# A graph layer bound by its gathers: first loads in one queue by need, two blocks' messages ahead of the weights, x + b_e copied one chunk in each block

## The chip, the cores and the metric

The kernel runs on one core of a Trainium2 chip. The metric is the device time of one execution in microseconds (us), of which a median over several runs is given. The profile is of one further execution. Engines are named as in the profile: PE is TensorE (PEld its weight loads), DVE is VectorE, ACT is ScalarE, POOL is GpSimd, SP is SyncE; SPq and ACTq stand for the DMA issues of SP and ACT.

## The reference

There are N = 8192 nodes of C = 256 channels and E = 131072 edges, sorted by destination. All data is fp32.

```python
ea = edge_attr @ w_e + b_e                       # 64 -> 256 per edge
msg = relu(x[src] + ea)
agg = segment_sum(msg, dst, num_segments=N)
t = x + agg
h_local = relu(t @ w1 + b1) @ w2 + b2
h_local = bn(h_local + x, bn1_g, bn1_b)
# attention inside groups of 32 nodes, 4 heads of 64
q, k, v = split((x.reshape(256, 32, 256) @ in_w.T + in_b), 3)
o = softmax(q k^T / 8) v
h_attn = bn(o @ out_w.T + out_b + x, bn2_g, bn2_b)
out = h_local + h_attn
out = out + (relu(out @ m_w1 + m_b1) @ m_w2 + m_b2)
result = layernorm(x + bn(out, bn3_g, bn3_b))
```

## The kernel before

**Edges.** The edges are worked in 128 blocks of 1024 (`NB`, `BE`). For a block, `gather` (L133) issues eight indirect DMAs from GpSimd (L138), each of 128 rows of 1 KB, into the buffer `xs`, of which there are four; `load_edges` (L148) issues four loads of 128 KB from SyncE into `ea` (two buffers). VectorE transposes `ea` into `eaT` (L169), TensorE multiplies by `w_e` into two two-bank PSUM tiles `pe` (L459), VectorE adds the gathered rows to make `msg` (L487, two instructions a block), and ScalarE applies the relu in place (L491). A gather of block b + 4 reuses the buffer of block b and so waits for the message of block b. `edge_hot` (L496) makes one-hot matrices, `edge_sums` (L510) and `edge_place` (L528, L538) sum two blocks' messages by destination and add them to the transposed nodes `xT`.

**x + b_e.** The bias `b_e` is added to all edges. For the first 20 blocks (`NX`) TensorE adds it with further matmuls into `pe` (L467), and the gathers read x itself. Meanwhile the kernel writes a copy xb = x + b_e to DRAM: load (L553), add on VectorE (L558), store (L559). From block 20 on gathers read xb and the matmuls at L467 fall away. The copies are cut by `steps` (L543): a step per two blocks, of one to three chunks of 512 nodes, in buffers shared with the dense layers. A step is loaded in one pair of blocks and added and stored in the next.

**Nodes.** The nodes are worked in 16 chunks of 512: `attention_front` (load xn at L276, transposes L283, q and k at L294), `attention_back` (v at L308, scores L325, softmax, output L360 and L372), and `dense` (all dense layers at L391, layernorm, store at L444). These generators are mixed into the blocks by `Work.run`, which spends a budget of estimated us per pair of blocks. Dense work begins only when all chunks are copied (`not xp_of`). The last 24 blocks are placed one by one with a list of expected gather times (`came`).

**Setup.** The source indices of the first two blocks come in by eight tiny loads (`srcd`, L64), so that GpSimd can start. Then the gathers and edge loads of blocks 0 and 1 are issued. All source indices are loaded as `srci_r` (L176), turned into fp32 (L193), transposed on TensorE (L197) and written to `srci` (L198), which gathers from block 2 on read. The destinations (`dsti_r`, L177) become `rel` and `wrow` (L232 to L267). Weights are transposed (L207).

**Order.** SyncE and ScalarE issue plain loads and stores; each of the two is one in-order queue, and across both eight completion semaphores are used in turn, so that a load waits for the one eight places before it to land. In the setup, a scheduler orders each engine's instructions. From the main loop on TensorE's order is as written (`manual_schedule`), and for the first 26 blocks (`NV`) VectorE's and ScalarE's as well (L661 to L667); after that the scheduler orders these two.

Of the kernel before, what the change touches and what calls it, by code (L numbers as in the profile page):

```python
# [18 lines left out]
P = 128  # L19
# [5 lines left out]
NH = 4  # L25
# [15 lines left out]
NV = 26  # L41
# [12 lines left out]
def gnn_kernel(ctx: ExitStack, tc: tile.TileContext, x, src, dst, edge_attr, w, out):  # L54
# [105 lines left out]
    load_edges(0)  # L160
    gather(1)
    load_edges(1)
# [7 lines left out]

    with tc.tile_pool(name="setup", bufs=1) as sp:


        srci_r = npool.tile([P, BE], I32, name="srci_r", tag="y")
        dsti_r = npool.tile([P, BE], I32, name="dsti_r", tag="h1")
        nc.sync.dma_start(srci_r, src.rearrange("(s e) -> s e", s=NB))  # L176
        nc.sync.dma_start(dsti_r, dst.rearrange("(s e) -> s e", s=NB))  # L177
        for h in range(2):
            nc.scalar.dma_start(we[h * ED : (h + 1) * ED, :], w["w_e"])
        nc.scalar.dma_start(be, w["b_e"][None, :].to_broadcast([P, C]))  # L180
        in_r = npool.tile([P, 3 * KC, C], FP, name="in_r", tag="m1")
        out_r = npool.tile([P, KC, C], FP, name="out_r", tag="vn")
        nc.scalar.dma_start(in_r, w["in_w"].rearrange("(o p) c -> p o c", p=P))
# [4 lines left out]
        nc.scalar.dma_start(out_r, w["out_w"].rearrange("(o p) c -> p o c", p=P))  # L188
        for b in range(2):
            edge_transpose(b)  # L190
            load_edges(b + 2)
        srcf = npool.tile([P, NH * TJ, EQ, QR], FP, name="srcf", tag="zT")
        nc.vector.tensor_copy(srcf, srci_r.rearrange("s (t r m) -> s t m r", r=QR, m=EQ))  # L193
        for h in range(NH):
            ps = bank()[:, : TJ * NB].rearrange("p (j s) -> p j s", j=TJ)
            for j in range(TJ):
                nc.tensor.transpose(ps[:, j, :], srcf[:, h * TJ + j].rearrange("s m r -> s (m r)"), ident)  # L197
            nc.vector.tensor_copy(srci[:, :, h * TJ : (h + 1) * TJ].rearrange("p s j -> p j s"), ps)  # L198

# [74 lines left out]
    def attention_front(n0, st, pool, bank):  # L274
        xn = st["xn"] = pool.tile([P, TN, C], FP, name="xn", tag="xn", bufs=4)
        nc.sync.dma_start(xn, x[ds(n0, CH), :].rearrange("(t p) c -> p t c", p=P))  # L276
        yield REST
# [170 lines left out]
    chunk = [{} for _ in range(NCH)]  # L448
    pe_of, msg_of, oh_of, newest = {}, {}, {}, {}

    def edge_products(b):

        eaT = eaT_of.pop(b).rearrange("p (h m) r -> p h (m r)", h=NH)
        for h in range(0, NH, 2):
            pe = bank2().rearrange("p i (u c) -> p i u c", u=2)
            for u in range(2):
                for i in range(2):
                    rows = slice(i * ED, (i + 1) * ED)
                    nc.tensor.matmul(  # L459
                        pe[:, i, u, :], eaT[rows, h + u], we[rows, :],  # L460
                        start=(b >= NX or u == 0), stop=(b >= NX), skip_group_check=True,
                    )
            if b < NX:
                for u in range(2):
                    for i in range(2):
                        rows = slice(i * ED, (i + 1) * ED)
                        nc.tensor.matmul(  # L467
                            pe[:, i, u, :], sel[rows, :], be[rows, :], start=False, stop=True, skip_group_check=True
                        )
            pe_of[b, h] = pe  # L470

    def next_edges(b):
        if b < NB:
            edge_transpose(b)
        if b + 2 < NB:
            load_edges(b + 2)

    def edge_messages(b):

        xs = xs_of.pop(b)  # L480
        msg = msg_of[b] = epool.tile([P, NH, TJ, C], FP, name="msg", tag="msg", bufs=3)
        n = 2 if b < NB - 1 else 1
        for h in range(0, NH, 2):
            pe = pe_of.pop((b, h))
            for u in range(0, 2, n):
                hs = slice(h + u, h + u + n)
                nc.vector.tensor_add(  # L487
                    msg[:, hs].rearrange("p u i c -> p i u c"), pe[:, :, u : u + n, :],
                    xs[:, hs].rearrange("p u i c -> p i u c"),
                )  # L490
                nc.scalar.activation(msg[:, hs], msg[:, hs], AF.Relu)  # L491

    def edge_hot(b):

        oh = oh_of[b] = epool.tile([P, TB, WN], FP, name="oh", tag="oh", bufs=2)
        nc.vector.tensor_tensor(  # L496
            oh,
            iota_n[:, None, :WN].to_broadcast([P, TB, WN]),
            rel[:, b, :, None].to_broadcast([P, TB, WN]),
            ALU.is_equal,  # L500
        )

    def edge_sums(blocks):

        pw = pps.tile([P, 2, C], FP, name="pw", tag="pw", bufs=1)
        for i, b in enumerate(blocks):
            msg, oh = msg_of.pop(b), oh_of.pop(b)
            for j in range(TJ):
                for h in range(NH):
                    nc.tensor.matmul(  # L510
                        pw[h * WN : (h + 1) * WN, i, :], oh[:, h * TJ + j, :], msg[:, h, j, :],
                        start=(j == 0), stop=(j == TJ - 1), skip_group_check=True,
                    )
        n = len(blocks)
# [3 lines left out]
        for i, b in enumerate(blocks):  # L518
            nc.vector.tensor_scalar(oh2[:, i, :], iota_n, wrow[:, b : b + 1], None, ALU.is_equal)
# [106 lines left out]
    with tc.manual_schedule(engines={PE}):  # L626
# [38 lines left out]
        while b < TAIL:  # L665
            if b == NV:
                early.close()  # L667
# [199 lines left out]
```

## Time and profile before

| what | value |
|---|---|
| median of 3 runs | 1328.58 us (1327.78 to 1329.9) |
| the profiled execution | 1331.09 us |
| its span | 1329.3 us |
| PE busy | 1195.2 us, 90% |
| POOL busy | 983.9 us, 74% |
| DVE busy | 784.9 us, 59% |
| ACT busy | 587.7 us, 44% |
| mean granted TensorE clock | 0.967 |
| DMA moved | 240.34 MB, mean 181 GB/s |

The span lies inside the profiled execution's own time. A row of a group reads: line, engine, operation, output and inputs, count, then total busy us and mean ns of one, then the engine's idle time just before these instructions and what ended most of it. A row of the order of time reads: start, duration, engine, line, operation, names, count, and in brackets the idle time just before and its releaser. Releasers are inferred; "issue" means that nothing which the profile shows was waited for. Successive instructions of one group are merged into one row.

### The profile page before, as it was taken

To read this page: it belongs to the slowest core of one execution; us is meant where nothing else is said; L and a number is where in the kernel's file an instruction comes from. 1 tells how busy PE (TensorE), PEld (TensorE's weight loads), DVE (VectorE), ACT (ScalarE), POOL (GpSimd) and SP (SyncE) were. 2 spreads that over 40 slices of the span, in tenths; PEclk is the share of its full clock that TensorE was granted. 3 is DMA by queue.
4 is the path that set the end of the run, shared out by engine and by line. 5 is a ranking of instruction groups with operands and counts; after the bars stand their busy time and mean duration, and the time that the engine had idled before them with its cause. 6 is when DMAs were issued, how large, how long until landed. Compare 5 with 4: busy or idle time off the path is not lost.

```text
span 1329.3 us, 21099 instructions
## 1 busy us (share of the span) xinstructions
PE 1195.2 (90%) x7795; PEld 741.0 (56%) x7795; DVE 784.9 (59%) x1339; ACT 587.7 (44%) x840; POOL 983.9 (74%) x1032
## 2 busy tenths in 40 slices
PE   2898989999998989899898988989898999999987
PEld 1566656556555556555555555545555555545655
DVE  4377555765756565755647465465646557575654
ACT  1343433454536454443435444354454444443433
POOL 6677777777777777777777777777777777777771
PEclk9899999999999989999999999989899999999998
DMA  7999966676667666666756666566566466656741
GB/s 204 320 267 299 260 199 169 169 199 167 181 160 196 157 181 167 171 177 165 190 150 185 160 176 171 157 181 167 170 169 199 138 169 186 166 163 159 192 129 47
DMA packets 148904, 240.34 MB, mean 181 GB/s; under 512 B 27934, under 2 KB 112188, under 8 KB 148028
## 3 DMA queue, kind: packets, MB, share of 16 engines
q0 software_dynamic: 49152, 134.28, 37.6%
q1 hardware_dynamic: 97196, 103.34, 28.9%
q10 hardware_dynamic: 2448, 1.32, 0.4%
q8 instruction: 63, 1.03, 0.3%
q14 instruction: 45, 0.37, 0.1%
HBM read 222.06 MB, written 16.78 MB: 180 GB/s over the span
## 4 chain that ended last, share of the span: by engine, by line
PE 38%; POOL 28%; issue 14%; DVE 9%; DMA 8%; ACT 2%; DVEq 0%; ACTq 0%; SPq 0%; POOLq 0%
POOL xs L138 28%; PE at L391 11%; PE pe L459 8%; DMA xs<-xb,srci 5%; PE at L294 5%; PE pw L510 4%; DVE msg L487 3%; PE l L528 3%; PE at L372 2%; PE pe L467 2%; PE at L308 1%; DMA xp<-in_x_dram 1%; PE at L360 1%; PE pe L325 1%; DMA in_r<-in_L_gnn_in_w_dram 1%
## 5 line engine op out<-in xcount | busy, mean ns | idle before, releaser
L138 POOL DMA_INDIRECT xs<-xb,srci x864 | 823.7, 953 | 263.2 <-issue 250.1
L491 ACT ACTIVATE msg<-msg 128x1024 f32<-128x1024 f32 (+1 forms) x258 | 270.0, 1049 | 435.5 <-DVE msg L487 432.6
L487 DVE TENSOR_TENSOR msg<-pe,xs 128x1024 f32<-128x1024 f32 (+1 forms) x258 | 305.7, 1199 | 155.4 <-DMA xs<-xb,srci 88.6
L459 PE MATMUL pe<-we,eaT 64*128 64x256 f32 x2048 | 271.0, 398 | 29.8 <-DVE msg L487 26.4
L459 PEld LDWEIGHTS pe<-we,eaT 64*128 64x128 f32 x2048 | 192.1, 191 | 118.5 <-issue 74.6
L138 POOL DMA_INDIRECT xs<-in_x_dram,srci x144 | 143.0, 993 | 48.8 <-issue 39.6
L169 DVE STREAM_TRANSPOSE eaT<-ea 128x512 f32<-128x512 f32 x128 | 90.1, 704 | 99.6 <-PE pe L459 70.9
L510 PE MATMUL pw<-msg,oh 128*32 128x256 f32 x2048 | 130.4, 389 | 6.6 <-DVE oh L496 5.0
L391 PE MATMUL at<-hA,mw 128*128 128x512 f32 (+2 forms) x304 | 123.9, 538 | 2.9 <-DVE hA L401 2.2
L294 PE MATMUL at<-xT,inT 128*128 128x512 f32 x256 | 120.9, 598 | 0.4 <-ACT xT L284 0.4
L391 PE MATMUL at<-m,mw 128*128 128x512 f32 (+2 forms) x304 | 117.5, 529 | 2.5 <-ACT qk L297 2.2
L510 PEld LDWEIGHTS pw<-msg,oh 128*32 128x32 f32 x2048 | 60.4, 111 | 69.1 <-issue 30.7
L528 PEld LDWEIGHTS l<-oh,ws 128*128 128x128 f32 x512 | 78.0, 196 | 28.4 <-issue 21.9
L528 PE MATMUL l<-oh,ws 128*128 128x160 f32 x512 | 87.9, 312 | 2.0 <-ACT ws L516 2.0
L391 PEld LDWEIGHTS at<-hA,mw 128*128 128x128 f32 x304 | 54.7, 196 | 50.5 <-issue 42.6
L391 PEld LDWEIGHTS at<-m,mw 128*128 128x128 f32 x304 | 54.2, 190 | 49.9 <-issue 44.5
L538 DVE TENSOR_TENSOR xT<-l,xT 128x96 f32<-128x96 f32 (+4 forms) x107 | 46.1, 452 | 54.2 <-PE l L528 53.9
L294 PEld LDWEIGHTS at<-xT,inT 128*128 128x128 f32 x256 | 47.0, 190 | 55.3 <-issue 51.0
L391 PE MATMUL at<-xT,w 128*128 128x512 f32 (+2 forms) x152 | 70.9, 606 | 6.9 <-DVE xT L538 6.9
L407 ACT ACTIVATE m<-at,vec 128x512 f32<-128x512 f32 (+2 forms) x76 | 46.8, 616 | 57.2 <-PE at L391 56.7
L297 ACT ACTIVATE qk<-at,vec 128x512 f32<-128x512 f32 x64 | 43.6, 684 | 62.6 <-PE at L294 62.4
L391 PE MATMUL at<-h,w 128*128 128x512 f32 (+2 forms) x152 | 64.2, 544 | 6.1 <-ACT h L398 6.1
(107 smaller groups left out, 1199.9 us busy)
## 6 DMA issues: line engine op xcount, KB each, us to landing
ea<-in_edge_attr_dram SPq DMA_DIRECT2D x512, 128.0 KB
xs<-xb,srci POOLq DMA_INDIRECT x864
xn<-in_x_dram SPq DMA_DIRECT2D x16, 512.0 KB
out_dram<-y SPq DMA_DIRECT2D x14, 512.0 KB
xp<-in_x_dram SPq DMA_DIRECT2D x10, 512.0 KB
xb<-xp SPq DMA_DIRECT2D x10, 512.0 KB
xp<-in_x_dram SPq DMA_DIRECT2D x3, 1024.0 KB
xb<-xp SPq DMA_DIRECT2D x3, 1024.0 KB
```

The lines of the kernel that those rows point to most:

```text
L138: nc.gpsimd.indirect_dma_start(out=xs[:, h, j, :], out_offset=None, in_=x if b < NX else xb[:, :], in_offset=bass.IndirectOffsetOnAxis(ap= ...
L169: nc.vector.transpose(eaT, ea[:, QR:].rearrange("p (g d) -> p g d", d=ED)[:, :, :QR])
L294: nc.tensor.matmul(ps, inT[:, k, o * P : (o + 1) * P], xT[:, k, :], start=(k == 0), stop=(k == KC - 1))
L297: nc.scalar.activation(qk[:, o, :], ps, AF.Identity, bias=v_("in_b", o))
L391: nc.tensor.matmul(ps, wt[:, k, o * P : (o + 1) * P], act[:, k, :], start=(k == 0), stop=(k == nk - 1))
L407: nc.scalar.activation(m1[:, o, :], layer(mw1, KC, o, hA), AF.Relu, bias=v_("m_b1", o))
L459: nc.tensor.matmul(pe[:, i, u, :], eaT[rows, h + u], we[rows, :], start=(b >= NX or u == 0), stop=(b >= NX), skip_group_check=True,)
L487: nc.vector.tensor_add(msg[:, hs].rearrange("p u i c -> p i u c"), pe[:, :, u : u + n, :], xs[:, hs].rearrange("p u i c -> p i u c"),)
L491: nc.scalar.activation(msg[:, hs], msg[:, hs], AF.Relu)
L510: nc.tensor.matmul(pw[h * WN : (h + 1) * WN, i, :], oh[:, h * TJ + j, :], msg[:, h, j, :], start=(j == 0), stop=(j == TJ - 1), skip_group_ ...
L528: nc.tensor.matmul(l2[:, k, i * NPB : i * NPB + WB], ws[:, i, k * P : (k + 1) * P], oh2[:, i, :], start=(i == 0 and k == 0), stop=(i == la ...
L538: newest["xT"] = nc.vector.tensor_add(xT, l2[:, :, a - n : z - n], xT).ins
```

## The change

Three things change in the order of the work; what is computed stays the same.

1. The first loads all go through SyncE, in this order: `srcd` (ScalarE still issues half of these), `srci_r`, edge loads of block 0, `w_e`, edge loads of block 1, `b_e`, `dsti_r`, the twelve vectors, `in_w`, nodes of chunk 0, `out_w`, nodes of chunk 1. Before, `srci_r` and `dsti_r` stood behind both blocks' edge loads, and ScalarE issued the weights.
2. The products and messages of blocks 0 and 1 are written in the setup, behind the index transposes and ahead of the weight transposes, where the scheduler orders the engines. The main loop leaves them out for these two blocks.
3. The copy of x + b_e goes by one chunk of 512 nodes in each block (`copy_step`), in four buffers in turn: load chunk i, add and store chunk i - 2. There are sixteen adds of 128x1024 where there were ten of that size and three of 128x2048.

Beside this the written order of VectorE and ScalarE in the first 26 blocks is taken out: the scheduler orders both throughout. TensorE's order stays written. The functions of the edge blocks move up in the file unchanged.

```diff
-NV = 26
...
     gather(0)
-    load_edges(0)
     gather(1)
-    load_edges(1)
...
+    def load_nodes(n0, st, pool):
+        xn = st["xn"] = pool.tile([P, TN, C], FP, name="xn", tag="xn", bufs=4)
+        nc.sync.dma_start(xn, x[ds(n0, CH), :].rearrange("(t p) c -> p t c", p=P))
...
         srci_r = npool.tile([P, BE], I32, name="srci_r", tag="y")
+        nc.sync.dma_start(srci_r, src.rearrange("(s e) -> s e", s=NB))
+        load_edges(0)
         dsti_r = npool.tile([P, BE], I32, name="dsti_r", tag="h1")
-        nc.sync.dma_start(srci_r, src.rearrange("(s e) -> s e", s=NB))
+        for h in range(2):
+            nc.sync.dma_start(we[h * ED : (h + 1) * ED, :], w["w_e"])
+        load_edges(1)
+        nc.sync.dma_start(be, w["b_e"][None, :].to_broadcast([P, C]))
         nc.sync.dma_start(dsti_r, dst.rearrange("(s e) -> s e", s=NB))
-        for h in range(2):
-            nc.scalar.dma_start(we[h * ED : (h + 1) * ED, :], w["w_e"])
-        nc.scalar.dma_start(be, w["b_e"][None, :].to_broadcast([P, C]))
...
-        nc.scalar.dma_start(in_r, w["in_w"].rearrange("(o p) c -> p o c", p=P))
         vec_r = npool.tile([nrows, P], FP, name="vec_r", tag="pr")
...
-        nc.scalar.dma_start(out_r, w["out_w"].rearrange("(o p) c -> p o c", p=P))
-        for b in range(2):
-            edge_transpose(b)
-            load_edges(b + 2)
+        nc.sync.dma_start(in_r, w["in_w"].rearrange("(o p) c -> p o c", p=P))
+        load_nodes(0, chunk[0], npool)
+        nc.sync.dma_start(out_r, w["out_w"].rearrange("(o p) c -> p o c", p=P))
+        load_nodes(CH, chunk[1], npool)
...
+        for b in range(2):
+            edge_transpose(b)
+            load_edges(b + 2)
+        edge_products(0)
+        next_edges(2)
+        edge_messages(0)
+        edge_products(1)
+        next_edges(3)
+        edge_messages(1)
...
-    steps = [[("m1", 0, 2), ("y", 2, 1)], [("h1", 3, 1), ("zT", 4, 1)], [("m1", 5, 2), ("y", 7, 1)],
-             [("h1", 8, 1), ("zT", 9, 1)], [("m1", 10, 2), ("y", 12, 1)], [("h1", 13, 1), ("zT", 14, 1)],
-             [("y", 15, 1)]]
...
+    XP = ("y", "h1", "zT", "m1")
...
+    def copy_step(i):
+
+        if i - 2 in xp_of:
+            xp = xp_of.pop(i - 2)
+            nc.vector.tensor_add(xp, xp, be[:, None, :].to_broadcast([P, TN, C]))
+            nc.sync.dma_start(rows(xb, i - 2), xp)
+        if i < NCH:
+            xp = xp_of[i] = npool.tile([P, TN, C], FP, name="xp", tag=XP[i % len(XP)])
+            nc.sync.dma_start(xp, rows(x, i))
...
-        early = ExitStack()
-        early.enter_context(tc.manual_schedule(engines={mybir.EngineType.DVE, mybir.EngineType.Activation}))
...
-            if b == NV:
-                early.close()
...
-            edge_products(b)
-            next_edges(b + 2)
-            edge_messages(b)
+            if b:
+                edge_products(b)
+                next_edges(b + 2)
+                edge_messages(b)
...
             work.run(0.3 * per)
-            copy_store(b // 2 - 1)
-            copy_load(b // 2)
+            copy_step(b)
             if sums:
                 edge_place(*sums)
                 placed, sums = sums[0][-1], None
             work.run(0.2 * per)
+            copy_step(b + 1)
```

## The prediction

> **What bounds the kernel now.** I first looked at engine totals, then at the costliest group, then at the waits of its engine and at single instructions in order of time.
>
> ```profile
> span 1329.3 us, 21099 instructions
> PE 1195.2 (90%) x7795; PEld 741.0 (56%) x7795; DVE 784.9 (59%) x1339; ACT 587.7 (44%) x840; POOL 983.9 (74%) x1032
> L138 POOL DMA_INDIRECT xs<-xb,srci x864 | 823.7, 953 | 263.2 <-issue 250.1
> ```
>
> TensorE looks like the bound at 90%, but it is not what sets the end. The gathers at L138 (GpSimd, "POOL") are 1024: 128 blocks of eight. Each takes 0.95 us, and 0.30 us of "issue" (waiting for nothing) lies before it. In order of time:
>
> ```profile
> 4.25 1.10 POOL L138 DMA_INDIRECT xs<-in_x_dram,srcd  x1 [2.65 <-issue]
> ...
> 1302.79 0.95 POOL L138 DMA_INDIRECT xs<-xb,srci  x1 [0.30 <-issue]
> ```
>
> From first to last gather are 1298.5 us. 1023 steps of 1.25 us are 1278.8 us, so only 19.8 us of this stretch is anything else. After it come 26.5 us of tail (1329.3 - 1302.8): the last landing, its message, sums and dense layers. A change of first loads and copies can win from the 19.8 us, not from TensorE's load. GpSimd's own waits name the large pieces:
>
> ```profile
> POOL xs L138 <- issue: 297.0, 967, 2.6
> POOL xs L138 <- DVE msg L487: 6.9, 13, 3.2
> ...
> POOL xs L138 <- DVE oh L519: 2.6, 4, 1.7
> ...
> POOL xs L138 <- DVE srci L198: 0.9, 1, 0.9
> ```
>
> (columns: total, times, longest). Nearly every other entry is the usual 0.30 us with a chance neighbour as releaser; I take the chain's long TensorE stretch before 880 us for the same, since no gather there starts late. The gathers that do:
>
> ```profile
> 23.16 1.80 POOL L138 DMA_INDIRECT xs<-in_x_dram,srcd  x1 [0.30 <-issue]
> 25.87 1.47 POOL L138 DMA_INDIRECT xs<-in_x_dram,srci  x1 [0.92 <-DVE srci L198]
> ...
> 49.30 0.94 POOL L138 DMA_INDIRECT xs<-in_x_dram,srci  x1 [3.22 <-DVE msg L487]
> ...
> 73.19 2.29 POOL L138 DMA_INDIRECT xs<-in_x_dram,srci  x1 [0.30 <-issue]
> ...
> 197.06 0.96 POOL L138 DMA_INDIRECT xs<-in_x_dram,srci  x1 [1.68 <-DVE oh L519]
> ```
>
> Above the normal 0.95 + 0.30: 2.0 us for the pair at 23-27 us; 2.9 us at 49.3 (first gather of block 4: the buffer of block 0 is released by its message); 1.4 us at 197.1 (block 18 waits for block 14's message); and long gathers like the one at 73.19, below. After 217 us nothing exceeds 0.5 us.
>
> **The change part by part.**
>
> *srci_r first in the queue.* Before, SyncE issued it at 15.26 us, behind eight edge loads, and it landed at 23.0; the indices were ready 2.6 us later, 0.6 us too late. Afterwards only the srcd loads stand before it: issue at 2.7, landing of its 512 KB by some 10 us (the DMA moved about 250 GB/s at 7.5-10 us, gathers included), indices by 13, needed at 24.4. The 0.62 us wait goes. The rest of the 2.0 us is two stretched gathers: 0.85 beside the conversion at L193, 0.52 beside the one at L232. Both conversions still run under gathers at another phase: 1.07 us each against a period of 1.25 hits with chance 0.86, for half its length, 0.46 each. 2.0 becomes 0.9: **-1.1 us**.
>
> *Messages of blocks 0 and 1 ahead of the weights.* Why was block 0's message late?
>
> ```profile
> 46.08 0.71 DVE L169 STREAM_TRANSPOSE eaT<-ea 128x512 f32<-128x512 f32 x1 [10.11 <-DMA xp<-in_x_dram]
> 46.72 1.19 DVE L487 TENSOR_TENSOR msg<-pe,xs 128x1024 f32<-128x1024 f32 x1
> ```
>
> In the order written out for VectorE it stood behind the edge transpose of block 2, whose data came at 46 us through a DMA full of 2.5 MB of xp loads. Now products and messages 0 and 1 stand behind edge loads 0 and 1, be and dsti_r alone: bytes before them 2.4 MB at the 110-145 GB/s that gathers (128 KB per 1.25 us, 105 GB/s) leave of 215-250 give landing at about 21 us, message 0 by 26, message 1 by 31. They are needed at 45 and 55. **-2.9 us.** What is late next: vec_r, in_r, xn stand behind dsti_r in one in-order queue, and the vec_r loads wait for earlier landings (the queue waited 5.1 us for in_r in one piece before). I put in_r at 27, xn at 29 and 33 us, the first attention matmuls at 38; before they began at 51.70. So TensorE and VectorE enter block 2 some 13 us earlier. TensorE then needs about 20 us per pair of blocks (messages of blocks 2, 4, 6, 8 at 64.0, 84.2, 103.0, 123.3), as gathers do, so the lead lasts.
>
> *The wait at 197 us.* Block 14's message ended at 196.7; 13 us earlier it is far before the gather wants it. **-1.4 us.** If all but 1.4 us of the lead were lost on the way, it would stay.
>
> *One chunk per block.* Before, ten adds of 128x1024 and three of 128x2048 (L558) stood in seven groups; now 16 of 128x1024. What VectorE pays (16 x 1.2 = 19.2 us against 18.7) is hidden. What GpSimd pays is not:
>
> ```profile
> 72.39 3.41 DVE L558 TENSOR_TENSOR xp<-xp,be 128x2048 f32<-128x2048 f32 x2
> ...
> 180.85 2.34 DVE L558 TENSOR_TENSOR xp<-xp,be 128x1024 f32<-128x1024 f32 x2
> ```
>
> The gather at 73.19 began inside the first add and ended 0.88 us after that add's end; the one begun at 180.93 took 1.95 us and also ended 0.88 us after the first add of its group. So a gather that starts under this add stands until the add ends; an add directly behind catches none, since the next gather starts 1.25 us later and the add lasts 1.13. The groups cost 1.35, 0.39, 1.10, 0.12, 1.30, 1.01 and 0: 5.3 us. In the changed program's instruction order the adds stand apart but for three in one place: 14 events. Worked out, each hits with chance 0.9 for half of 1.13, 0.51: 7.1 us; the four groups with a 1024 add in front averaged 0.38: 5.3 us. I take 0.44: 6.2 us, **+0.9 us**; ends 3 and 10 us. The Trainium skill's page "SBUF — State Buffer" (section "Who interferes with whom") says of an elementwise add with two SBUF inputs that it contends only with GpSimd work that reads SBUF, and infers from a probe in which such an add stalled no DMA that generating descriptors needs the write side alone. By that inference the copies cost nothing before or after, and the sum lacks the +0.9. The seven groups above decide against it (a gather also reads its indices from SBUF, which may be the point at which it stands; no row shows that).
>
> *Nothing for the rest.* ScalarE's five DMA issues of weights go to SyncE: ScalarE was idle then. VectorE's and ScalarE's order is no longer written out for blocks 0-25: TensorE's order is that of before from block 2 on but for a few pieces of 1.7 us that trade places, and identical for the last quarter, as are VectorE's and ScalarE's last 400 and 260 instructions, so I leave the 26.5 us tail. xb is complete earlier (the last add stands behind message 11, before behind 15), so block 20's gather doesn't wait. The other long gathers (some 8 us in small pieces) stay; their phases may move this by 1.5 either way.
>
> Sum: -1.1 - 2.9 - 1.4 + 0.9 = **-4.5 us**; span 1329.3 to 1324.8, its execution 1331.1 to 1326.6. The median of the runs shown, 1328.58, lies 2.5 us under the profiled one; from it I get **1324.1 us** (-0.34%).
>
> **Rivals.** *Adds in front of messages.* In the new VectorE order adds 11 and 12 precede message 10 and add 13 its second half; an add whose load hasn't landed holds the message, xs isn't released, and block 14's first gather (due at 4.25 + 112 x 1.25 + about 7 = 151 us) stands. Copy traffic is squeezed: 14 loads and 11 stores of 0.52 MB, edge loads of ten blocks (0.52 MB each), 1.6 MB of weights and 1.0 of xn, 20.9 MB, from about 41 us.
>
> ```profile
> GB/s 204 320 267 299 260 199 169 169 199 167 181 160 196 157 181 167 171 177 165 190 150 185 160 176 171 157 181 167 170 169 199 138 169 186 166 163 159 192 129 47
> ```
>
> Slices 2 to 4 (33-133 us) average 295; less 105 for gathers (128 KB per 1.25 us) leaves 190, so 20.9 MB end at 151: no margin. For it: one in-order queue, where an xp load waits for a store and edge loads stand behind. Against it: while xp loads ran (40-47 us) the DMA moved 390 GB/s, so copies are cheaper bytes than the average. It decides the sign when add 13 is over 4.5 us late, below 182 GB/s; at 175 it is 9 us late, time 1333.
>
> *No gain that counts.* Adds cost 10 us instead of 6.2 and the order leaves 1.4 us of waiting: -4.5 + 3.8 + 1.4 = +0.7; with half of each, 1326.7.
>
> *More.* Adds fall as luckily as 3 us, other stretched gathers 1.5 less: -9.2, 1319.4.
>
> *The change doesn't do it:* message 0 still late, since dsti_r's reductions stand before it. It would need 20 us more than worked out; 3 in 100.
>
> **How the numbers follow.** A change under 0.2% (2.7 us) can't be told from none here. Main case 0.60 (1324.1, own range 1321.5-1326.5), no gain that counts 0.16, late adds 0.15 (1325 to 1335), more 0.06, change ineffective 0.03. Main case beyond -2.7 us about 0.87: 0.52; with "more" and the mild end of late adds 0.62. Same: 0.08 + 0.13 + a little of late adds = 0.24. Slower 0.14. Range 1320.5 to 1329.5: below lies half of "more" and little else, above the worse half of late adds.
>
> **What would show it.** Right: block 0's message before 30 us; no gather with over 0.31 us idle before it at blocks 2, 4, 18; single gathers of up to 2.1 us beside the add, 4 to 8 us in all; last gather at 1298 us, tail 26.5. Wrong: idle time on GpSimd near 150 us released by a message that followed an add; another tail.

## The result and the profile after

The change makes the kernel slower by 0.4%: 1333.81 us (median of 14 runs, 1331.17 to 1337.10) against 1328.57 us of the kernel before on the same chip (14 runs, 1325.87 to 1331.38), ratio 1.0040 with a 95% interval of 1.0029 to 1.0052. The forecast was 1324.1 us, range 1320.5 to 1329.5. The measured time is outside the range and of the other sign. The profiled execution of the changed kernel took 1333.48 us, near its median; that of the kernel before (1331.09) lay at the upper end of its runs, so the spans differ by less than the medians.

The page of the changed kernel (engine totals, then the two large groups of gathers):

```profile
span 1331.6 us, 21087 instructions
PE 1195.6 (90%) x7795; PEld 744.3 (56%) x7795; DVE 785.9 (59%) x1342; ACT 585.8 (44%) x838; POOL 984.7 (74%) x1032
...
L137 POOL DMA_INDIRECT xs<-xb,srci x864 | 821.5, 951 | 269.6 <-issue 244.3
...
L137 POOL DMA_INDIRECT xs<-in_x_dram,srci x144 | 145.6, 1011 | 43.9 <-issue 41.4
```

The engine totals say nothing: TensorE has the same 1195 us of work. Compared with before, the idle time ahead of the xb gathers went from 263.2 to 269.6 us, and the mean of the other gathers from 993 to 1011 ns. GpSimd in order of time:

```profile
4.27 1.10 POOL L137 DMA_INDIRECT xs<-in_x_dram,srcd  x1 [2.67 <-issue]
...
22.90 1.17 POOL L137 DMA_INDIRECT xs<-in_x_dram,srcd  x1 [0.30 <-issue]
24.37 0.95 POOL L137 DMA_INDIRECT xs<-in_x_dram,srcd  x1 [0.30 <-issue]
25.62 0.94 POOL L137 DMA_INDIRECT xs<-in_x_dram,srci  x1 [0.30 <-issue]
...
46.16 0.94 POOL L137 DMA_INDIRECT xs<-in_x_dram,srci  x1 [0.30 <-issue]
...
195.02 1.06 POOL L137 DMA_INDIRECT xs<-in_x_dram,srci  x1 [0.30 <-issue]
...
233.87 0.95 POOL L137 DMA_INDIRECT xs<-xb,srci  x1 [0.30 <-issue]
241.49 0.94 POOL L137 DMA_INDIRECT xs<-xb,srci  x1 [6.67 <-DVE msg L207]
...
1305.03 0.94 POOL L137 DMA_INDIRECT xs<-xb,srci  x1 [0.30 <-issue]
```

All three waits that the forecast removes are gone: block 2's first gather (25.62), block 4's (46.16) and block 18's (195.02) have only the usual 0.30 us before them. What is new is one wait of 6.67 us before block 22's first gather at 241.49. That gather reuses the buffer of block 18, and block 18's message is late.

The table cuts the gather stretch at the first gathers of six blocks. Each entry is the time between two of these starts less 1.25 us for each gather. It is used for all kernels below; the labels are those of the experiments.

| kernel | blocks 0-2 | 3-4 | 5-17 | 18-19 | 20-21 | 22-127 | sum |
|---|---|---|---|---|---|---|---|
| before | 2.2 | 3.0 | 7.6 | 0.0 | 0.0 | 7.0 | 19.8 |
| forecast for after | 1.1 | 0.1 | 7.1 | 0.0 | 0.0 | 7.0 | 15.3 |
| after | 1.4 | 0.5 | 8.9 | 0.1 | **6.4** | 4.8 | 22.0 |
| after, second profile | 1.4 | 0.4 | 8.7 | 0.0 | **4.5** | 7.8 | 22.9 |
| E1 TensorE's old order | 1.7 | 0.5 | 9.0 | 0.0 | 0.4 | 7.5 | 19.1 |
| E2 order written | 2.1 | 0.0 | 6.7 | **17.3** | 0.0 | 7.2 | 33.2 |
| E3 before, dense later | 1.0 | 3.4 | 7.6 | 0.0 | **7.5** | 5.8 | 25.3 |
| E4 = E1 and E2 | 1.2 | 0.5 | 6.0 | **7.1** | 0.2 | 7.4 | 22.4 |
| E5 parts 1 and 2 alone | 2.1 | 0.4 | 5.3 | 0.2 | 0.1 | 6.2 | 14.2 |
| E5u same, order left open | 2.0 | 0.0 | **12.2** | 0.0 | 1.1 | 5.9 | 21.2 |
| E6 copies sooner | 1.9 | 0.1 | **10.9** | 0.0 | 0.0 | 5.6 | 18.5 |
| E7 = E6 without adds | 1.6 | 0.5 | 0.2 | 0.0 | 0.1 | 6.8 | 9.2 |

Each column runs to the first gather of the block after it. So the wait before block 2 lies in "0-2", that before block 4 in "3-4", before block 18 in "5-17", before block 20 in "18-19" and before block 22 in "20-21". The last column moves by 3 us between two executions of one program, so differences of that size in a sum are not read.

**Why message 18 is late.** TensorE of the changed kernel in order of time, around the wait:

```profile
217.24 1.16 PE L434 MATMUL pe<-qk 64*128 64x128 f32 x16 [0.59 <-DVE msg L207]
218.34 1.35 PE L248 MATMUL l<-oh,ws 128*128 128x160 f32 x8
219.53 1.88 PE L500 MATMUL at<-xT,w 128*128 128x512 f32 x4
227.94 3.68 PE L469 MATMUL at<-bd,vn 128*64 128x128 f32 x32 [6.53 <-DVE bd L461]
231.55 3.03 PE L500 MATMUL at<-xT,w 128*128 128x512 f32 x4
...
236.22 1.14 PE L179 MATMUL pe<-we,eaT 64*128 64x256 f32 x8
```

VectorE in the same stretch:

```profile
225.03 2.85 DVE L461 STREAM_TRANSPOSE bd<-pr 32x512 f32<-32x512 f32 x4
236.34 0.75 DVE L484 SCALAR_TENSOR_TENSOR hA<-at,s,hA 128x512 f32<-128x512 f32 x1 [8.46 <-PE at L481]
238.27 1.22 DVE L207 TENSOR_TENSOR msg<-pe,xs 128x1024 f32<-128x1024 f32 x1 [1.18 <-PE pe L187]
239.41 0.70 DVE L166 STREAM_TRANSPOSE eaT<-ea 128x512 f32<-128x512 f32 x1
240.04 1.18 DVE L207 TENSOR_TENSOR msg<-pe,xs 128x1024 f32<-128x1024 f32 x1
```

TensorE computes attention scores (L434), then sums of messages (L248) and one dense piece (L500), and then its order wants the attention output (L469). Between scores and output lies the softmax, which VectorE finishes at 227.9. TensorE stands 6.53 us, and the edge products of block 18 (L179 at 236.22), which need nothing of the softmax, stand behind it in order. Their message ends at 241.2, and 0.3 us later GpSimd goes on. The kernel before in the same stretch:

```profile
223.78 1.88 PE L391 MATMUL at<-h,w 128*128 128x512 f32 x4
225.59 2.06 PE L325 MATMUL pe<-qk 64*128 64x128 f32 x32
228.34 1.14 PE L459 MATMUL pe<-we,eaT 64*128 64x256 f32 x8 [0.69 <-ACT pr L335]
```

There the scores come last in pair 16 (blocks 16 and 17), the edge products of block 18 follow at once, and the attention output of this chunk comes only in pair 20, at 255.3 us.

What moved it is one condition. Dense work may begin when no copy is left (`not xp_of`), and that is decided where TensorE's order is written, not when the kernel runs. The copies by steps end in the middle of pair 14; the copies by one chunk a block end with `copy_step(17)`, in pair 16, though their last add in fact runs at 161 us where it was 202 us before. So in pairs 14 and 16 there is no dense work to put between the pieces of the attention, scores and output move together, and TensorE's order differs from the old one in 35 of the 64 pairs, all from pair 14 on.

### The profile page after: what moved, and what is told of

It is laid out like the page before. It is cut to its first block, busy times and chain, and to the rows that moved or that the text cites. A ratio compares the mean times of both kernels' runs of the same rounds, so it can differ in the third digit from the quotient of the medians.

```text
span 1331.6 us, 21087 instructions
## 1 busy us (share of the span) xinstructions
PE 1195.6 (90%) x7795; PEld 744.3 (56%) x7795; DVE 785.9 (59%) x1342; ACT 585.8 (44%) x838; POOL 984.7 (74%) x1032
## 4 chain that ended last, share of the span: by engine, by line
PE 39%; POOL 25%; issue 13%; DVE 10%; DMA 8%; ACT 4%; DVEq 0%; SPq 0%; ACTq 0%; POOLq 0%
POOL xs L137 25%; PE at L500 13%; PE pe L179 8%; DMA xs<-xb,srci 4%; PE pw L230 4%; PE at L403 4%; DVE msg L207 3%; PE l L248 3%; PE at L417 2%; PE at L481 2%; ACT pr L444 1%; PE pe L434 1%; DMA xs<-in_x_dram,srci 1%; DMA xp<-in_x_dram 1%; DVE bd L461 1%
## 5 line engine op out<-in xcount | busy, mean ns | idle before, releaser
L137 POOL DMA_INDIRECT xs<-xb,srci x864 | 821.5, 951 | 269.6 <-issue 244.3
L207 DVE TENSOR_TENSOR msg<-pe,xs 128x1024 f32<-128x1024 f32 (+1 forms) x258 | 307.8, 1200 | 150.6 <-DMA xs<-xb,srci 77.6
L179 PE MATMUL pe<-we,eaT 64*128 64x256 f32 x2048 | 269.8, 398 | 42.1 <-DVE msg L207 36.9
L179 PEld LDWEIGHTS pe<-we,eaT 64*128 64x128 f32 x2048 | 190.1, 190 | 132.6 <-issue 56.8
L137 POOL DMA_INDIRECT xs<-in_x_dram,srci x144 | 145.6, 1011 | 43.9 <-issue 41.4
L230 PE MATMUL pw<-msg,oh 128*32 128x256 f32 x2048 | 127.6, 383 | 1.4 <-ACT msg L211 0.8
L500 PE MATMUL at<-hA,mw 128*128 128x512 f32 (+2 forms) x304 | 122.8, 532 | 1.2 <-DVE hA L510 1.1
L500 PE MATMUL at<-m,mw 128*128 128x512 f32 (+2 forms) x304 | 117.4, 529 | 0.3
L248 PEld LDWEIGHTS l<-oh,ws 128*128 128x128 f32 x512 | 79.1, 198 | 29.5 <-issue 23.2
L248 PE MATMUL l<-oh,ws 128*128 128x160 f32 x512 | 89.0, 315 | 1.7 <-ACT ws L236 1.6
L500 PEld LDWEIGHTS at<-hA,mw 128*128 128x128 f32 x304 | 53.8, 190 | 51.5 <-issue 43.3
L500 PEld LDWEIGHTS at<-m,mw 128*128 128x128 f32 x304 | 54.6, 191 | 48.0 <-issue 44.9
L500 PE MATMUL at<-xT,w 128*128 128x512 f32 (+2 forms) x152 | 67.4, 578 | 7.7 <-DVE xT L258 6.9
L500 PE MATMUL at<-h,w 128*128 128x512 f32 (+2 forms) x152 | 64.3, 544 | 8.3 <-ACT h L507 5.2
```

Source lines behind the costliest of these rows:

```text
L137: nc.gpsimd.indirect_dma_start(out=xs[:, h, j, :], out_offset=None, in_=x if b < NX else xb[:, :], in_offset=bass.IndirectOffsetOnAxis(ap= ...
L179: nc.tensor.matmul(pe[:, i, u, :], eaT[rows, h + u], we[rows, :], start=(b >= NX or u == 0), stop=(b >= NX), skip_group_check=True,)
L207: nc.vector.tensor_add(msg[:, hs].rearrange("p u i c -> p i u c"), pe[:, :, u : u + n, :], xs[:, hs].rearrange("p u i c -> p i u c"),)
L230: nc.tensor.matmul(pw[h * WN : (h + 1) * WN, i, :], oh[:, h * TJ + j, :], msg[:, h, j, :], start=(j == 0), stop=(j == TJ - 1), skip_group_ ...
L248: nc.tensor.matmul(l2[:, k, i * NPB : i * NPB + WB], ws[:, i, k * P : (k + 1) * P], oh2[:, i, :], start=(i == 0 and k == 0), stop=(i == la ...
L500: nc.tensor.matmul(ps, wt[:, k, o * P : (o + 1) * P], act[:, k, :], start=(k == 0), stop=(k == nk - 1))
```

## The experiments

The runs E1 to E4 shared one chip (before: 1329.41 us), E5 to E7 a second (1329.28), E5u and the repeat of the changed kernel a third (1329.05).

**E1: the changed kernel with TensorE's old order.** The step that loads the last chunk (`copy_step(15)`) comes one place earlier, and dense work may begin at the place in pair 14 where it began before. TensorE's order is then that of the kernel before from block 2 on; all else is as changed.

```diff
+    begun = []
...
-            return lambda: placed >= last and chunk[c].get("done") and not xp_of and b > 2
+            return lambda: placed >= last and chunk[c].get("done") and begun
...
             copy_step(b)
+            if b == 14:
+                copy_step(15)
+                begun.append(b)
...
-            copy_step(b + 1)
+            if b != 14:
+                copy_step(b + 1)
```

> The changed kernel with one thing undone: dense work may begin in the pair of blocks 14 as in the kernel before, so that TensorE's written order from block 2 on is exactly that of before; loads, early messages, copies and the scheduler's order of VectorE and ScalarE stay. Theory A (TensorE's new order at blocks 16 to 19 puts the attention output right behind the scores, TensorE stands 6.5 us for the softmax, and message 18 releases its buffer late): the 6.37 us before the first gather of block 22 are gone, time 1325 to 1327.5. Theory B (adds waiting for their loads in front of messages used up the lead): the stall stays, 1332 to 1335.

Measured: 1330.77 us, ratio 1.0010 (1.0002 to 1.0018). E1 in order of time:

```profile
222.39 2.06 PE L434 MATMUL pe<-qk 64*128 64x128 f32 x32
225.53 1.13 PE L179 MATMUL pe<-we,eaT 64*128 64x256 f32 x8 [1.08 <-ACT pr L444]
...
234.56 0.95 POOL L137 DMA_INDIRECT xs<-xb,srci  x1 [0.30 <-issue]
235.81 0.95 POOL L137 DMA_INDIRECT xs<-xb,srci  x1 [0.30 <-issue]
```

Block 22's first gather (235.81) no longer waits. Of the +0.40% of the change, 0.30% is gone. But E1 is slower than the expected 1325 to 1327.5 us and not faster than before, where the forecast wanted -0.34% of just this: something else is missing.

**E3: the kernel before with TensorE's new order.** Only the start of dense work is put off to the last third of pair 16.

```diff
+    late = [False]
...
-            return lambda: placed >= last and chunk[c].get("done") and not xp_of and b > 2
+            return lambda: placed >= last and chunk[c].get("done") and not xp_of and late[0]
...
             work.run(0.2 * per)
+            late[0] = late[0] or b >= 16
```

> The kernel before with only the start of dense work put off to the last third of the pair of blocks 16, which gives exactly the changed kernel's TensorE order; loads, messages, copies and the written order of VectorE and ScalarE stay as before. Theory A: TensorE stands about 6 us for the softmax near 220 us and the first gather of block 22 comes 3 to 7 us late (message 18 had 2.9 us to spare), 1331 to 1336. Theory B: no difference, 1327.5 to 1329.5.

Measured: 1334.98 us, ratio 1.0049 (1.0035 to 1.0064). First loads, messages, copies and the written orders of VectorE and ScalarE are those of before, and the same wait appears. E3 in order of time:

```profile
229.70 3.68 PE L360 MATMUL at<-bd,vn 128*64 128x128 f32 x32 [6.49 <-DVE bd L352]
...
235.56 0.94 POOL L138 DMA_INDIRECT xs<-xb,srci  x1 [0.30 <-issue]
243.79 0.96 POOL L138 DMA_INDIRECT xs<-xb,srci  x1 [7.29 <-DVE oh L519]
```

Message 18 ends at 243.5 us here, 0.3 us before the gather; the one-hot matrix (`oh`) that the row names as releaser is VectorE's next instruction. With E1 this shows the cause of the wait from both sides: TensorE's order alone makes it, and undoing that order alone takes it away.

**E2: the changed kernel with VectorE's and ScalarE's order written for blocks 2 to 25.** TensorE's order stays the new one.

```diff
+        early = ExitStack()
+        early.enter_context(tc.manual_schedule(engines={mybir.EngineType.DVE, mybir.EngineType.Activation}))
...
+            if b == 26:
+                early.close()
```

> The changed kernel with VectorE's and ScalarE's order written out again for blocks 2 to 25, as before; TensorE's order as in the changed kernel. Theory A: TensorE's wait for the softmax at blocks 16 to 19 stays and with it a stall of GpSimd at block 22, 1330 to 1335. Theory B: adds stand behind both messages of a pair again, TensorE keeps its lead of 13 us at block 2, the wait is absorbed, no stall at block 22, 1323 to 1327.

Measured: 1341.50 us, ratio 1.0090 (1.0075 to 1.0105). E2 in order of time:

```profile
223.66 3.68 PE L469 MATMUL at<-bd,vn 128*64 128x128 f32 x32 [6.49 <-DVE bd L461]
...
223.64 1.23 DVE L568 TENSOR_TENSOR xp<-xp,be 128x1024 f32<-128x1024 f32 x1
224.78 0.68 DVE L258 TENSOR_TENSOR xT<-l,xT 128x352 f32<-128x352 f32 x2
225.38 1.21 DVE L568 TENSOR_TENSOR xp<-xp,be 128x1024 f32<-128x1024 f32 x1
...
213.19 0.95 POOL L137 DMA_INDIRECT xs<-in_x_dram,srci  x1 [0.30 <-issue]
230.38 0.94 POOL L137 DMA_INDIRECT xs<-xb,srci  x1 [16.25 <-issue]
```

This is slower than either theory expected. TensorE's wait for the softmax is there (6.49 us), but GpSimd stands earlier, at block 20. The last two adds now stand behind the softmax in VectorE's written order. The last one ends at 226.6; block 20's gather, the first that reads xb, was due at 214.4 and comes at 230.38, 3.8 us after that add. The row names no releaser; that it waits for the last copy's store is read from the program. The scheduler, left free, had put the last add at 161 us.

**E4: E1 and E2 together.**

> Both undone: TensorE's order from block 2 on and VectorE's and ScalarE's in blocks 2 to 25 as before; first loads, early messages and one chunk per block stay. Theory A: as the one with TensorE's order alone, within 1.5 us, 1324 to 1327.5. Theory B: as the one with VectorE's order alone. If the sum of the prediction holds once no order differs: 1323 to 1326.

Measured: 1333.16 us, ratio 1.0027 (1.0017 to 1.0038). This too is slower than each expectation (1323 to 1327.5 us). There is no wait at block 22, but block 20 still waits: the last add ends at 215.3 us, and the gather comes 3.7 us later, so the last copy is again the likely releaser (E4 in order of time):

```profile
211.56 1.80 POOL L137 DMA_INDIRECT xs<-in_x_dram,srci  x1 [0.30 <-issue]
218.96 0.94 POOL L137 DMA_INDIRECT xs<-xb,srci  x1 [5.60 <-issue]
```

E4 also shows what became of the lead. Ends of four messages, in us (E5 to E7 are described below):

| message of block | 2 | 6 | 10 | 14 |
|---|---|---|---|---|
| before | 66.4 | 105.3 | 150.6 | 196.8 |
| after (order left open) | 53.8 | 104.3 | 152.3 | 194.2 |
| after, second profile (order left open) | 53.9 | 101.6 | 148.2 | 192.5 |
| E1 (order left open) | 55.0 | 103.6 | 151.0 | 192.7 |
| E5u (order left open, copies by steps) | 55.7 | 99.4 | 153.9 | 196.9 |
| E4 (order written) | 54.8 | 94.3 | 140.1 | 186.3 |
| E5 (order written, copies by steps) | 54.5 | 93.5 | 140.0 | 186.9 |
| E6 (order written, copies sooner) | 56.2 | 102.8 | 150.0 | 196.9 |
| E7 (as E6, no adds) | 55.2 | 94.1 | 139.5 | 186.1 |

Between 10 and 13 us are won at block 2 by all of them. In E4, E5 and E7 some 10 us are left at block 14; with the order left open at most 2.4 us are left at block 10. In the changed kernel the lead falls from 8.7 us at block 4 (77.8 against 86.5) to 1.0 us at block 6, and one add shows why: it waits for its load, 6.77 us, between the two halves of message 6. The changed kernel's group of adds (idle time of VectorE before them, us and times) and, in order of time, block 6:

```profile
L568 DVE TENSOR_TENSOR xp<-xp,be x16: 1181/1225/1227, 57.6 to 161.3; 128x1024 f32<-128x1024 f32 x16
...
  DMA xp<-in_x_dram: 24.8, 9
...
93.33 1.22 DVE L207 TENSOR_TENSOR msg<-pe,xs 128x1024 f32<-128x1024 f32 x1
94.46 0.70 DVE L166 STREAM_TRANSPOSE eaT<-ea 128x512 f32<-128x512 f32 x1
101.93 1.23 DVE L568 TENSOR_TENSOR xp<-xp,be 128x1024 f32<-128x1024 f32 x1 [6.77 <-DMA xp<-in_x_dram]
103.07 1.22 DVE L207 TENSOR_TENSOR msg<-pe,xs 128x1024 f32<-128x1024 f32 x1
```

Nine such waits take 24.8 us of VectorE; before, and in E4, no add waited for its load.

**E5: parts 1 and 2 alone.** The copies go by steps and VectorE's and ScalarE's order is written again for blocks 2 to 25, as before; the first loads and the early messages are as changed.

```diff
-    XP = ("y", "h1", "zT", "m1")
+    steps = [[("m1", 0, 2), ("y", 2, 1)], [("h1", 3, 1), ("zT", 4, 1)], ...
...
+        early.enter_context(tc.manual_schedule(engines={mybir.EngineType.DVE, mybir.EngineType.Activation}))
...
-            copy_step(b)
+            copy_store(b // 2 - 1)
+            copy_load(b // 2)
...
-            copy_step(b + 1)
```

> The kernel with the first two parts alone, on a chip whose TensorE isn't held back. Theory A (lateness on GpSimd alone sets the time): 4 to 6 us under the kernel before, no gather with over 0.31 us idle before it at blocks 2, 4 and 18. Rival (another gather waits instead): within 2 us of the kernel before.

Measured: 1325.96 us, ratio 0.9972 (0.9962 to 0.9982): the fastest of all kernels that do the whole work. The page of E5:

```profile
span 1322.3 us, 21098 instructions
...
L137 POOL DMA_INDIRECT xs<-xb,srci x864 | 822.9, 952 | 263.3 <-issue 246.6
...
L137 POOL DMA_INDIRECT xs<-in_x_dram,srci x144 | 142.0, 986 | 43.9 <-issue 40.2
```

No gather waits anywhere (43.9 us before 144 gathers is 0.30 each). The gather stretch is 5.6 us shorter than before, where these two parts and the wait at block 18 were put at 5.4; but the median is only 3.3 us shorter, less than the expected 4 to 6.

**E5u: E5 with the order left open.** The edit of E5 without the written order.

> As the one with the first two parts alone, VectorE's and ScalarE's order left to the scheduler throughout, on a chip whose TensorE isn't held back. If that order costs by itself (adds in front of messages, the lead used up): 2 to 6 us above the one with the order written out (3.3 us under the kernel before). If it costs only together with one chunk per block: within 1.5 us of it.

Measured: 1330.83 us, ratio 1.0011 (1.0002 to 1.0019). Leaving VectorE and ScalarE to the scheduler, with the old copies, costs 0.39% and undoes the whole gain. E5u in order of time:

```profile
94.68 2.70 POOL L137 DMA_INDIRECT xs<-in_x_dram,srci  x1 [0.30 <-issue]
...
94.27 2.29 DVE L574 TENSOR_TENSOR xp<-xp,be 128x2048 f32<-128x2048 f32 x1 [2.49 <-DMA xp<-in_x_dram]
```

The gather starts 0.41 us into an add of 2.29 us and ends 0.82 us after it. Three gathers of 2.6 to 3.0 us lie beside the three large adds. In the written order the adds of a step stood back to back and only the first could catch a gather (forecast's reading); the scheduler sets them apart. Gathers stretched beside an add cost 11.1 us in E5u, 4.3 in E5, 5.2 before.

**E6 and E7: copies sooner, with and without the adds.** E6 is the changed kernel with the order written and a third copy step in pairs 2, 4 and 6, so that the copies end in pair 14 and dense work begins there by the unchanged rule. E7 leaves the sixteen adds out of E6 (the last line of the diff below): the gathers from block 20 on then read rows without `b_e`.

```diff
...
-            copy_step(b)
+            copy_step(b + extra)
...
-            copy_step(b + 1)
+            copy_step(b + extra + 1)
             for i in blocks:
                 edge_hot(i)
+            if b in (2, 4, 6):
+                extra += 1
+                copy_step(b + extra + 1)
...
-            nc.vector.tensor_add(xp, xp, be[:, None, :].to_broadcast([P, TN, C]))
```

> The kernel with the third step in the pairs 2, 4 and 6, on a chip whose TensorE isn't held back. Theory A: no stall on GpSimd, 3 to 4.5 us under the kernel before, adds costing GpSimd 6 to 8 us. Rival (copies of this size hold messages wherever they are written): a stall of over 2 us at blocks 12 to 20, no better than the kernel before.

> As the one with a third step in the pairs 2, 4 and 6, with the sixteen adds of b_e left out (the copy holds x alone, so gathers from block 20 on lack b_e), on a chip whose TensorE isn't held back. If the adds stall gathers by 5 to 8 us in all and GpSimd sets the time: 5 to 8 us under the kernel with the adds. If an add with two SBUF inputs stalls no gather, as the Trainium skill's page infers: within 1 us of it.

Measured: E6 1327.74 us, ratio 0.9986 (0.9980 to 0.9992); E7 1318.91 us, ratio 0.9912 (0.9899 to 0.9925), 8.8 us less. The gathers between 40 and 195 us (count, then shortest, median and longest in ns), of E6:

```profile
L137 POOL DMA_INDIRECT xs<-in_x_dram,srci x117: 942/946/1906, 39.9 to 193.7; - x117
```

and of E7:

```profile
L137 POOL DMA_INDIRECT xs<-in_x_dram,srci x124: 942/947/983, 40.1 to 194.0; - x124
```

Without the adds no gather in this stretch takes longer than 0.98 us, and seven more of them fit in. E6's two waits (1.2 us before block 16, 2.2 us before block 18) are gone as well. So the adds do hold the gathers: of what they cost E6, 3.4 us are the two waits, the rest stretched gathers. E6 itself fell between its two expectations. Its message of block 14 ends at 196.9, no earlier than before, though its order is written, and again it is the adds: ahead of the softmax that precedes message 4 stand three of them in VectorE's order, the third (at 70.6 us) after 3.4 us of waiting for its load, and message 4 ends at 81.5 us. E7 has the same loads and stores, its message 4 ends at 74.7 us, and its lead lasts.

**The same four kernels on two chips with a lower granted clock.** E5, E6, E7 and E5u were first run on two other chips, where the granted TensorE clock was about 0.82 instead of 0.96 and the kernel before took 1998.85 and 2029.45 us.

Expected on the first, in the order E5, E6, E7, E5u:

> The kernel before with the first two parts alone: first loads in one queue by need, and the products and messages of blocks 0 and 1 in the setup. Copies by steps and the written order of VectorE and ScalarE (from block 2) as before; TensorE's order from block 2 on that of before. Theory A (lateness on GpSimd alone sets the time; these two parts take 1.1, 2.9 and 1.4 us of it): 4 to 6 us under the kernel before, no gather with over 0.31 us idle before it at blocks 2, 4 and 18. Rival (the 13 us of lead are needed elsewhere or lost, and another gather waits): within 2 us of the kernel before.

> One chunk at a time, but a third step in the pairs of blocks 2, 4 and 6, so that the last chunk is added in the pair 14, where dense work may then begin by the unchanged rule; VectorE's and ScalarE's order written out for blocks 2 to 25. TensorE's order from block 2 on is that of before. Theory A (what was left after TensorE's order was undone is the wait of block 20 for the copy, 5.6 us, which this takes away): no stall, 3 to 4.5 us under the kernel before, the adds costing GpSimd 6 to 8 us. Rival (copies of this size hold messages wherever they are written): a stall of over 2 us at blocks 12 to 20, no better than the kernel before.

> As the one with a third step in the pairs 2, 4 and 6, with the sixteen adds of b_e left out (the copy holds x alone, so gathers from block 20 on lack b_e): same loads, stores and orders otherwise. If the adds stall gathers by 7 us in all: 6 to 8 us under the kernel with the adds. If an add with two SBUF inputs stalls no gather, as the Trainium skill's page infers: within 1 us of it.

> As the one with the first two parts alone, but VectorE's and ScalarE's order left to the scheduler throughout. If leaving the order to the scheduler costs by itself (adds in front of messages, the lead used up): 2 to 6 us above the one with the order written out. If it costs only together with one chunk per block: within 1.5 us of it.

Expected on the second, in the same order:

> The kernel with the first two parts alone once more, on a chip on which the kernel before takes its usual time. Theory A (lateness on GpSimd alone sets the time): 4 to 6 us under the kernel before, no gather with over 0.31 us idle before it at blocks 2, 4 and 18. Rival (another gather waits instead): within 2 us of the kernel before.

> The kernel with the third step in the pairs 2, 4 and 6 once more. Theory A: no stall on GpSimd, 3 to 4.5 us under the kernel before, adds costing GpSimd 6 to 8 us. Rival (copies of this size hold messages wherever they are written): a stall of over 2 us at blocks 12 to 20, no better than the kernel before.

> As the one with a third step in the pairs 2, 4 and 6, with the sixteen adds of b_e left out (the copy holds x alone, so gathers from block 20 on lack b_e), once more. On the chip where TensorE set the time the stretched gathers added up to 8.3 us with the adds and 3.1 us without. If the adds stall gathers by 5 to 8 us in all and GpSimd sets the time: 5 to 8 us under the kernel with the adds. If an add with two SBUF inputs stalls no gather, as the Trainium skill's page infers: within 1 us of it.

> The kernel with the first two parts and VectorE's and ScalarE's order left to the scheduler throughout, once more. If that order costs by itself (adds in front of messages, the lead used up): 2 to 6 us above the one with the order written out. If it costs only together with one chunk per block: within 1.5 us of it.

Measured, as ratios to the kernel before, on the first and second of these chips: E5 1.0020 (0.998 to 1.006) and 0.9975 (0.995 to 1.000), E6 1.0052 (1.0025 to 1.0079) and 1.0093 (1.0061 to 1.0125), E7 1.0126 (1.0075 to 1.0178) and 1.0079 (1.0051 to 1.0107), E5u 1.0009 (0.9981 to 1.0038) and 1.0037 (1.0007 to 1.0068). No expected gain is clear of the noise. In E7's profile on the first of them GpSimd is busy 48% of the span instead of 74%, and 515 us of its waits end with a message (6.9 us in the kernel before on the usual chip). The gathers there wait for the messages and do not set the time, so these runs don't speak to the question.

**The changed kernel once more**, beside E5u:

> The changed kernel itself once more beside it, on the same chip: 5 us above the kernel before, with a stall of 5 to 10 us before the first gather of block 22.

Measured: 1334.15 us, ratio 1.0040 (1.0029 to 1.0050), as on the first chip. Its profile has the wait before block 22 again, with 4.5 us in place of 6.4.

## Why the prediction was wrong

From the ratios, in us against 1329: the forecast is -4.5, the measurement +5.3, a miss of 9.8. E1 stands at +1.3 and E5 at -3.7. So the miss splits into 4.0 (after to E1: TensorE's order), 4.1 (E1 to E5, 5.0, of which the forecast had 0.9: copies by chunk and order left open) and 1.7 (E5's -3.7 instead of -5.4: the size of parts 1 and 2).

- *What bounds the kernel.* Right. The large differences show up in the gather stretch, at the places in order of time that the table names, while TensorE's busy time stays at 1191 to 1205 us and does not follow the span.
- *srci_r first*, -1.1: block 2's wait is gone, and blocks 0-2 went from 2.2 to 1.4 us. But this stretch was 1.0 us in E3 with the old loads and 1.2 to 2.1 us in others with the new ones, so the gain can't be told from the chance of the stretched gathers in it.
- *Messages ahead of the weights*, -2.9, and *the wait at 197 us*, -1.4: right, block 0's message ended at 22.1 us (forecast: by 26), and both waits are gone. The 12.6 us that block 2's message is earlier answer to the 13 of the forecast.
- *One chunk per block*, +0.9: the mechanism is right, shown by E7 against E6, and the inference on the Trainium skill's page "SBUF — State Buffer" (section "Who interferes with whom"), by which these adds stall no descriptor generation, does not carry over to these gathers; whether they stand in that or in reading their indices from SBUF, no run separates. The size was low: in the trace gathers beside the adds cost 7.4 us, not 6.2. (The 8.8 us that E7 wins contain E6's two waits.)
- *Nothing for the rest* is the step that failed, twice over. First, it held that "TensorE's order is that of before from block 2 on but for a few pieces of 1.7 us that trade places". It was 35 of 64 pairs. The moved pieces themselves cost nothing, TensorE's busy time being the same. But a written order is also a chain of waits, and with the pieces went the distance between attention scores and attention output. The question was not what the moved pieces cost but which dependent pair they had kept apart. E1 and E3 show it: TensorE stands 6.5 us for the softmax, GpSimd 4.5 to 7.0 us more than usual for message 18, and the order is worth 4.0 us of the time. Second, it gave no price to leaving VectorE's and ScalarE's order open: E5u against E5 puts it at 5.2 us with copies by steps, where gathers beside the adds cost 11.1 us instead of 4.3. E1, with copies by chunk, is no slower than E5u, so with the order left open no cost of the chunks themselves needs to be added. What they cost with the order written stays open: no run changes them alone, and E6, whose copies also come sooner, is 1.8 us slower than E5.
- *"So the lead lasts."* Failed in the changed kernel, held with the order written in E4, E5 and E7 (second table). The rival "adds in front of messages" saw the mechanism: an add whose load is late holds a message. It looked for the damage at block 14 by 151 us. There message 10 ended at 152.3 and the gather came at 153.7, so nothing was lost. The mechanism left no slack in its place, and 0.8 us before block 18, and then the 6.5 us of TensorE at block 18 hit GpSimd almost in full. Whether the lead, kept, would have covered them is open: E2, which keeps most of it with TensorE's new order, waits earlier, at block 20, for its last copy.
- *The tail stays.* 26.6 us against 26.5; in the repeat 23.4.

Two differences between profile and median are largely those of single executions. E1 is faster than the changed kernel by 0.30% (4.0 us) in the median, while the wait in the profile is 6.4 us; in the repeat it is 4.5 us. E5's gain in the median is 2 us smaller than in its gather stretch, but the profiled execution of the kernel before lay 2.5 us above its median and E5's 1.8 us below.

One rival is untested: the granted TensorE clock. On the chips where the kernel takes 1329 us, the kernel before was granted 0.967 to 0.968 (medians of its runs), the kernels with the early messages 0.957 to 0.963. Among the 22 runs of E6 a clock lower by 0.001 goes with 0.4 us more (correlation -0.77), among the 16 of the repeat with 0.7 us (-0.78); the runs of the kernel before show no such relation (-0.25 to +0.28). No run sets the clock, so which of the two follows the other is open. If the time followed the clock, some 2 us of each comparison with the kernel before would be due to it (an estimate, 0.005 at E6's slope), as much as is missing from E5's gain. The comparisons on which the cause rests (after with E1, E1 with E5, E5 with E5u, E6 with E7) are between kernels granted 0.960 to 0.963; E3 shows the wait at 0.9645.

## What to carry to other kernels

When the order of an engine is written out by a planner, look for every condition that the planner asks while it writes (here: "all copies done"), and follow what a moved condition does to pairs of dependent pieces; compare the two orders by the distance between producer and consumer, not by the sum of what moved. A change that bundles several edits is best priced edit by edit: here the first two win 0.28% alone, and an order that was taken out with them gives it back. A lead won early has to be followed to the place where it is needed, and an engine that waits in order for a load uses it up.

## What the runs showed of the hardware

- A gather issued by GpSimd that starts under a VectorE add of two SBUF operands (128x1024 or 128x2048, fp32) stays until 0.81 to 0.83 us after the add's end: 1.91 us beside an add of 1.21 us (E6), 2.70 and 3.00 us beside adds of 2.29 us (E5u). In the ten profiles that have these adds at a clock of about 0.96, 107 gathers started under one with more than 0.15 us of it to go, and 106 of them ended so. A gather already under way when such an add begins is not held: none of 80 took over 1.01 us. Without the adds none of 124 gathers took more than 0.98 us (E7). So adds set apart can each hold a gather, where adds back to back held one between them (three adds from 125.61 us in the changed kernel, one gather of 1.97 us).
- Two of the chips granted TensorE a clock of 0.81 to 0.85 in every run, the others 0.955 to 0.974. The kernel takes 1999 to 2029 us there instead of 1329, far more than the ratio of the clocks; TensorE is busy 1430 of 2025 us in E7 on the first of them, so its lower clock alone does not account for the time, and what does is open. A comparison made on one kind of chip says little on the other.
